# The last batch's two query tiles in the other order, in a two-layer transformer kernel

## The chip, the cores and the metric

The kernel runs on one NeuronCore of a Trainium2 chip. The metric is the device time of one execution in microseconds (us). The kernel before took 961.02 us (median of three runs, 960.78 to 964.9).

TensorE (PE) multiplies matrices; VectorE (DVE), ScalarE (ACT) and GpSimd (POOL) do elementwise work, and the queue of SyncE (SP) issues most of the DMAs. Everything is float32.

## What is computed

Two post-norm layers on x of 4 batches x 256 tokens x 512 features. After every attention and every feed-forward product the residual is added and the sum is normalised over its features.

```python
x = _layernorm(x + _L0_attn_ref(x, Wq, bq, Wk, bk, Wv, bv, Wo, bo))  # causal, 32 heads of 16, 8 KV heads
x = _layernorm(x + _L0_ffn_ref(x, q_scales, q_vals, bias))           # x @ W.T + bias, W = scale * (q - 128)
x = _layernorm(x + _L1_attn_ref(x, w_qkv, w_o))                      # causal, 32 heads of 128, 8 KV heads, bias -slope * sqrt(distance)
x = _layernorm(x + _L1_ffn_ref(x, kernel))                           # x @ w, w made of one int8 row of weights, 8 times
```

Attention is causal. The 256 queries of a batch are cut into two tiles of 128. Query tile 0 sees 128 keys, query tile 1 sees all 256: for a query tile qt, the width is w = (qt + 1) * 128.

## The kernel before

**Tiles.** The 1024 tokens are 8 token tiles of 128 rows; token tile 2 * b + qt holds query tile qt of batch b. x (first the input, later x2, the output of layer 0) lies in 8 slots of one pool.

**Layer 0, attention.** The helper `run` (L325) walks over 64 steps (b, qt, h, i): 4 batches, 2 query tiles, 2 halves of the KV heads, 4 query heads per group. A group of 8 steps makes one query tile. At step n, `run` traces in this order:
- `before0` (L543): at the first step of a batch, the projections of the next batch are appended to the list `ahead`; batch 3 has none.
- `begin0` (L475) of step n: scores sc on PE (L484), causal mask (DVE, L489), negated maximum (DVE, L492), four exponentials with their sums (ACT, L276); then `divide0` for the step before: reciprocal of the sums (DVE, L281) and the division of the probabilities pr (POOL, L284).
- `fill` (L556): one piece of every tail that is open, and one piece of `ahead`.
- `transpose0` (L508) of step n - 3: transposes of pr (PE, L299), one PSUM bank per 128 keys, each copied out to prT by ACT or DVE in turn (L102, L104). prT has 5 slots; a group of query tile 0 takes 2 of them, one of query tile 1 takes 4.
- `end0` (L524) of step n - 5: after the last step of a group, the output o (PE, L532, 16 matmuls per 128 keys), its copy oT, and a new tail.

**Layer 0, tails.** `tail0` (L436) takes a token tile through output projection py (L440), residual and statistics (L442, L259 to L262, the power on POOL), normalise (L266) to x1, transposes to x1T, bias addition (POOL, L453), feed-forward product pf (L457), residual and statistics (L461), normalise to x2, transposes to x2T. Between the steps it yields; two idle yields are left out for the last token tile (L448, L467).

**The border.** After step 63 `run` goes on without scores: the division of the last step, the last transposes, the last o. Then come the early projections of layer 1 (`first`, L739), which read only the first 512 tokens, while the last two tails end. The later projections need sums of the four quarters of x2T, made on POOL by `token_sums` (L599): all token columns but those of the last tile in one call (L744), held behind the newest power on POOL, and the last tile's columns in another (L697).

**Layer 1.** `run` walks over 64 steps (kv, b, qt), with transposes one step and o two steps after the scores. For the KV heads 0 to 6 the transposes go through DVE and DMAs. For the last one, kv = 7, they are on PE (L299), and each o leads to `output1` (L838: py, L842) and `tail1` (L771): residual, statistics, the sums xs of four quarters of features, their transpose, product pf (L797), z (L799), statistics, and the output. The output of the last token tile is written in two halves from two queues (L808 to L813), that of the others in one DMA (L818). After the last step a loop (L1066) ends what is open.

**What sets the order.** [...]The framework's scheduler fills the queues at compile time: roughly in the order in which the program traces the instructions, though an instruction that it takes to be ready earlier can move ahead. `keep_in_program_order` and `issue_after` pin some of them. The feed-forward weight of layer 0 comes as int32 codes (qv, L152) and is decoded in place (wf_n, L210). It lies in the pool `wa`, beside layer 0's other weights. The pool `w1` holds the weights of layer 1, its output weight wo1 in two slots.

Of the kernel before, what the change touches and what calls it, by code (L numbers as in the profile page):

```python
# [12 lines left out]
F32 = mybir.dt.float32  # L13
I32 = mybir.dt.int32
# [6 lines left out]
P = 128  # L21
B, S, D = 4, 256, 512
NTT = B * S // P
NC = D // P
NKV, G = 8, 4
BLK = 32
# [16 lines left out]

def alibi_slopes():
# [13 lines left out]
def block_kernel(  # L62
# [26 lines left out]
    const = pool(ctx, "const")  # L89
    xp = pool(ctx, "xp", NTT)  # L90
    w1 = pool(ctx, "w1", 2)
# [16 lines left out]
    xf = x_in.flatten_outer_dims()  # L108
    for tt in range(NTT):
        x.append(xp.tile([P, D], F32, tag="x", name=f"x_{tt}"))  # L110
# [7 lines left out]
    table = const.tile([P, 2 * P], F32, name="table")  # L118
    x2T = const.tile([P, NC, B * S], F32, name="x2T")

# [3 lines left out]
    wa = pool(la, "wa", side="right")  # L124
# [11 lines left out]
    def bank_m(name):  # L136
        return ps_w.tile([P, D], F32, tag="w", name=name)


    wq_n = x2T[:, :, 0:D]  # L140
    wq = wa.tile([P, NC, G, P], F32, name="wq")
    wk = wa.tile([P, NC, P], F32, name="wk")
    wv = wa.tile([P, NC, P], F32, name="wv")
    wop = w0.tile([P, G, D], F32, name="wop")
# [4 lines left out]
    bo_b = wa.tile([P, D], F32, name="bo_b")  # L149
    fb_b = w0.tile([P, D], F32, name="fb_b")  # L150
    brow = wa.tile([G + 1, P], F32, name="brow")
    qv = wa.tile([P, NC, D], I32, name="qv")  # L152
    qs = wa.tile([P, NC, D // BLK], F32, name="qs")
    wf_n = qv.bitcast(F32)

    tc.keep_in_program_order(nc.scalar.dma_start(wk, Wk.rearrange("(c p) n -> p c n", p=P)))
    tc.keep_in_program_order(
# [18 lines left out]
    nc.sync.dma_start(fb_b, f_bias.partition_broadcast(P))  # L176
    for tt in range(4, NTT):
        nc.sync.dma_start(x[tt], xf[ts(tt, P), :])
# [257 lines left out]
    def tail0(tt, oT):  # L436

        py = bank_m(f"py_{tt}")
        for i in range(G):
            nc.tensor.matmul(py, oT[:, i, :], wop[:, i, :], start=(i == 0), stop=(i == G - 1))  # L440
        y = s0.tile([P, D], F32, tag="y", name=f"y_{tt}")
        nc.vector.tensor_tensor(y, py, x[tt], ALU.add)  # L442
        factors = norm_factors(y, f"a{tt}")
        yield True
        x1 = s0.tile([P, D], F32, tag="x1", name=f"x1_{tt}")
        normalise(x1, y, factors)
        yield True
        if tt < NTT - 1:  # L448
            yield True
            yield True  # L450
        x1T = s0.tile([P, NC, P], F32, tag="x1T", name=f"x1T_{tt}")
        transposed(x1T, x1, f"x1_{tt}")
        nc.gpsimd.tensor_tensor(x1, x1, fb_b, ALU.add)  # L453
        yield True
        pf = bank_m(f"pf_{tt}")
        for c in range(NC):
            nc.tensor.matmul(  # L457
                pf, x1T[:, c, :], wfT[:, c, :], start=(c == 0), stop=(c == NC - 1)
            )
        y2 = s0.tile([P, D], F32, tag="y", name=f"y2_{tt}")  # L460
        nc.vector.tensor_tensor(y2, pf, x1, ALU.add)  # L461
        factors = norm_factors(y2, f"b{tt}")
        yield True
        x2[tt] = xp.tile([P, D], F32, tag="x", name=f"x2_{tt}")
        normalise(x2[tt], y2, factors)
        yield True
        if tt < NTT - 1:  # L467
            yield True
            yield True
        transposed(x2T[:, :, ts(tt, P)], x2[tt], f"x2_{tt}")  # L470
        yield True
# [36 lines left out]
    def transpose0(b, qt, h, i, pr):  # L508
        name = f"0_{b}_{qt}_{h}_{i}"
        if i == 0:  # L510
            open0[h] = [
                a0.tile(
                    [P, G, 4, 4, 32], F32, tag="prT", name=f"prT0_{b}_{qt}_{h}_{kt}", bufs=5
                )
                for kt in range(qt + 1)
            ]
        transposed_probabilities(
            name,
            pr,
            [(kt, open0[h][kt][:, i].rearrange("p j n q -> p n j q")) for kt in range(qt + 1)],  # L520
        )
        return open0[0], open0[1] if h else None
# [19 lines left out]

    def before0(step):  # L543
        b, qt, h, i = step
        if (qt, h, i) == (0, 0, 0):
            if b == 0:
                for _ in range(3):
                    advance(ahead)
            else:
                exhaust(ahead)  # L550
            if b + 1 < B:
                ahead.append(project0(b + 1))
            if b == 1:
                load_weights1(0)

    def fill():  # L556
# [3 lines left out]
    ahead.append(project0(0))  # L560
    tails.append(feed_forward_weight())
    run(
        [(b, qt, h, i) for b in range(B) for qt in range(2) for h in range(2) for i in range(G)],
        begin0,
        transpose0,
        end0,
# [15 lines left out]
    qk1 = {}  # L582
    v1 = a1.tile([P, NTT, NKV * P], F32, name="v1", bufs=1)

# [14 lines left out]
    def token_sums(start, end):  # L599
        B11, B21, B12, B22 = (  # L600
            x2T[:, 2 * j : 2 * j + 2, h * D + start : h * D + end]
            for h in range(2)
            for j in range(2)
        )
        t2_, t3_, t4_ = (xt[:, n, :, start:end] for n in range(3))
        nc.gpsimd.tensor_tensor(t3_, B22, B12, ALU.subtract)
        nc.gpsimd.tensor_tensor(B12, B12, B11, ALU.subtract)
        nc.gpsimd.tensor_tensor(t2_, B22, B12, ALU.subtract)
        return nc.gpsimd.tensor_tensor(t4_, B21, t2_, ALU.subtract)
# [59 lines left out]
    def project1(kv):  # L669

        wq1, _ = weights1[kv]
        parts = []
        if kv % 2 == 0:
            wk1 = wk_pair[kv // 2]
            nc.scalar.mul(wk1, wk1, scale)
            for e in range(2):
                kT1[kv + e] = a1.tile([P, B * S], F32, tag="kT1", name=f"kT1_{kv + e}", bufs=3)
            C = {(e, h): kT1[kv + e][:, ts(h, D)] for e in range(2) for h in range(2)}
            parts.append(Quarters(f"k_{kv}", halves(wk1, P, 0, P), None, C))
        qT = a1.tile([P, G, B * S], F32, tag="qT1", name=f"qT1_{kv}")  # L680
        for n in range(2):
            C = {(i, h): qT[:, 2 * i + n, ts(h, D)] for i in range(2) for h in range(2)}
            A = halves(wq1, P, n * P, (2 + n) * P)
            parts.append(Quarters(f"q_{kv}_{n}", A, None, C))

        def sums(part, where=p1):
            ws = where.tile([P, 4, 2, P], F32, tag="ws", name=f"ws_{part.name}", bufs=1)
            part.S = [ws[:, m] for m in range(4)]
            left_sums(part.S, part.A)

        if kv == 0:
            for part in parts:
                yield from part.early()
            sums(parts[0])
            for part in value_parts:
                yield from part.early()
            complete = token_sums(3 * P, D)  # L697
        for n, part in enumerate(parts):
            if kv > 0:
                sums(part)  # L700
                yield from part.early()
            yield from part.late()
            if kv == 0 and n == 0:
                with tc.issue_after(complete.ins):
                    sums(parts[1], border["pool"])
            elif kv == 0 and n + 1 < len(parts):
                sums(parts[n + 1])
            if kv == 0 and n == 0:
                with tc.issue_after(complete.ins):
                    left_sums(value_parts[0].S, value_parts[0].A)  # L710
            if kv == 0 and n > 0:
                yield from value_parts[n - 1].late()
        if kv == 0:
            yield from value_parts[2].late()
            yield from value_parts[3].late()
        qk1[kv] = (qT, kT1[kv])
        yield True
# [22 lines left out]
    for n in range(7):  # L740
        advance_all(tails)
        if n == 2:
            with tc.issue_after(powers[-1].ins):
                token_sums(0, 3 * P)  # L744
        next(first)
    exhaust(tails)
    l0.close()
# [23 lines left out]
    def tail1(tt):  # L771
# [33 lines left out]
        nc.gpsimd.tensor_tensor(rs, rs, minus_half, ALU.pow)  # L805
        yo = t1.tile([P, D], F32, tag="yo", name=f"yo_{tt}")
        rows = out.flatten_outer_dims()[ts(tt, P), :]
        if tt == NTT - 1:  # L808
            for part, queue in zip((ts(0, 2 * P), ts(1, 2 * P)), (nc.sync, nc.scalar)):
                nc.vector.tensor_scalar(  # L810
                    yo[:, part], z[:, part], mv[:, 0:1], rs, ALU.subtract, ALU.mult
                )
                queue.dma_start(rows[:, part], yo[:, part])  # L813
        else:
            shift = t1.tile([P, 1], F32, tag="shift", name=f"shift_{tt}", bufs=4)
            nc.gpsimd.tensor_scalar(shift, mv[:, 0:1], rs, -1.0, ALU.mult, ALU.mult)
            nc.scalar.activation(yo, z, AF.Identity, bias=shift, scale=rs)
            nc.sync.dma_start(rows, yo)  # L818
# [227 lines left out]
    def fill1():  # L1046
# [7 lines left out]
            advance(ahead)  # L1054

    run(
        [(kv, b, qt) for kv in range(NKV) for b in range(B) for qt in range(2)],
        begin1,
        transpose1,
        end1,  # L1060
# [42 lines left out]
```

## Time and profile before

| what | value |
|---|---|
| the three timed runs | 960.78, 961.02, 964.9 us |
| the profiled execution | 960.96 us |
| its span, first to last instruction | 958.8 us |
| around the span | 2.2 us |
| mean granted TensorE clock | 0.992 |
| first scores of batch 3, layer 0 | 195.66 us |
| first instruction of the last py of layer 0 | 266.41 us |
| last py of layer 1 begins | 944.48 us |

All places in the profile are us from the span's start. A row of the timeline has its start, its length, engine, line, operation, output <- inputs, shapes and count; a bracket at the end has the engine's idle time before it and what ended that. A row of a table by stage has a stretch, its length, the busy us of each engine and the granted clock (1.00 is full speed).

### The profile page before, as it was taken

The numbers are of one execution on the slowest core, as the hardware profiler recorded it, in microseconds if no ns is written. First come the engines' busy times: TensorE is split into PE (matmuls) and PEld (weight loads), VectorE is DVE, ScalarE is ACT, GpSimd is POOL, SyncE is SP. The second block draws the span as 40 slices with busy tenths as digits, with TensorE's granted clock in tenths as the row PEclk, the third lists the DMA queues.
The fourth block names the chain that finished last, engine by engine and source line by source line (L and its number), as shares of the span: only waits on it lengthen the run. The fifth ranks groups of instructions, "written<-read, shape, count | busy, mean of one in ns | idle before, by whom it ended". The sixth has DMA issues, their size and how long they took to land.

```text
span 958.8 us, 11377 instructions
## 1 busy us (share of the span) xinstructions
PE 922.0 (96%) x3593; PEld 554.1 (58%) x3593; DVE 619.4 (65%) x1291; ACT 315.2 (33%) x1194; POOL 445.6 (46%) x461
## 2 busy tenths in 40 slices
PE   8999999998899999999999999999999999999996
PEld 5655455553544445666666666666666666666652
DVE  4886777778533447655667666666676576666566
ACT  3674555466411003232222222212122122214441
POOL 3563553554457015445443543534543534556732
PEclk9999999999899999999999999999999999999998
DMA  8500000000020102444443353343344333432001
GB/s 242 184 1 1 0 1 1 1 1 1 1 88 22 45 0 72 128 115 126 110 135 86 112 152 99 121 125 95 117 125 111 115 83 110 126 94 69 1 34 55
DMA packets 76418, 74.45 MB, mean 78 GB/s; under 512 B 5957, under 2 KB 52678, under 8 KB 76358
## 3 DMA queue, kind: packets, MB, share of 16 engines
q1 hardware_dynamic: 75014, 72.02, 26.2%
q10 hardware_dynamic: 1344, 1.70, 0.6%
q8 instruction: 29, 0.48, 0.2%
q14 instruction: 31, 0.25, 0.1%
HBM read 49.58 MB, written 24.12 MB: 77 GB/s over the span
## 4 chain that ended last, share of the span: by engine, by line
PE 79%; POOL 9%; DVE 6%; ACT 2%; issue 1%; DMA 1%; ACTq 0%; POOLq 0%; DVEq 0%
PE p_q L632 18%; PE po L881 14%; PE sc L968 7%; PE o L1008 7%; PE p_k L632 5%; PE p_v L632 5%; PE sc L484 4%; PE pt L299 3%; PE py L440 3%; PE pf L457 3%; PE o L532 2%; PE pq L401 2%; POOL pr L284 2%; ACT pr L276 2%; PE py L842 2%; POOL x L903 2%
## 5 line engine op out<-in xcount | busy, mean ns | idle before, releaser
L276 ACT ACTIVATE pr<-sc,nm 128x256 f32<-128x256 f32 (+1 forms) x512 | 209.5, 421 | 362.2 <-DVE nm L984 277.2
L284 POOL TENSOR_TENSOR pr<-pr,sums 128x512 f32<-128x512 f32 (+1 forms) x128 | 190.4, 1489 | 231.2 <-DVE sums L281 220.9
L976 DVE SCALAR_TENSOR_TENSOR sc<-table,sc 128x128 f32<-128x128 f32 (+1 forms) x256 | 86.1, 356 | 34.7 <-PE sc L968 32.4
L276 ACT ACTIVATION_READ_ACCUMULATOR pr<-sc,nm 128x1 f32 x512 | 104.2, 203 | 0.0
L968 PEld LDWEIGHTS sc<-kT,qT 128*128 128x128 f32 x512 | 82.3, 191 | 35.1 <-issue 29.7
L968 PE MATMUL sc<-kT,qT 128*128 128x256 f32 (+1 forms) x512 | 95.0, 327 | 0.0
L1008 PE MATMUL o<-prT,v 128*128 128x512 f32 x192 | 92.9, 592 | 0.0
L310 DVE STREAM_TRANSPOSE blocks<-pr 128x512 f32<-128x512 f32 x84 | 57.6, 698 | 45.2 <-POOL pr L284 45.1
L646 DVE TENSOR_TENSOR qT<-p_q,qT 128x512 f32<-128x512 f32 x96 | 64.6, 686 | 33.6 <-PE p_q L632 32.8
L299 PE MATMUL pt<-ident,pr 128*128 128x128 f32 x432 | 64.3, 284 | 11.7 <-POOL pr L284 8.2
L299 PEld LDWEIGHTS pt<-ident,pr 128*128 128x128 f32 x432 | 50.7, 145 | 38.1 <-issue 19.9
L984 DVE TENSOR_REDUCE nm<-sc 128x2 f32<-128x512 f32 (+1 forms) x128 | 70.1, 551 | 1.5
L484 PE MATMUL sc<-kT,qT 32*128 32x256 f32 (+1 forms) x256 | 61.6, 532 | 2.8 <-ACT pr L276 2.7
L492 DVE TENSOR_REDUCE nm<-sc 128x4 f32<-128x512 f32 (+1 forms) x64 | 61.0, 954 | 1.2
L881 PE MATMUL po<-wo,so 128*128 128x256 f32 x224 | 58.0, 381 | 2.1 <-POOL so L612 2.1
L632 PE MATMUL p_q<-x2T,ws_q 128*128 128x512 f32 x128 | 59.8, 592 | 0.0
L489 DVE TENSOR_TENSOR sc<-sc,causal 128x512 f32<-128x512 f32 x64 | 44.4, 694 | 22.8 <-PE sc L484 22.5
L104 ACT COPY o<-o 128x512 f32<-128x512 f32 x29 | 17.0, 586 | 124.9 <-PE o L1008 124.9
L632 PE MATMUL p_q<-xt,ws_q 128*128 128x512 f32 x128 | 57.7, 592 | 0.0
L881 PE MATMUL po<-wo,o 128*128 128x256 f32 x224 | 57.7, 380 | 0.0
L632 PE MATMUL p_q<-x2T,wq 128*128 128x512 f32 x128 | 57.6, 592 | 0.0
L881 PE MATMUL po<-to,so 128*128 128x256 f32 x224 | 53.3, 381 | 1.0 <-POOL so L615 1.0
(155 smaller groups left out, 1410.2 us busy)
## 6 DMA issues: line engine op xcount, KB each, us to landing
way<-blocks SPq DMA_DIRECT2D x112, 128.0 KB, 2.5
prT<-way SPq DMA_DIRECT2D x28, 512.0 KB, 3.7
wq<-in_L_attn_w_qkv_dram SPq DMA_DIRECT2D x8, 1024.0 KB, 5.1
wo<-in_L_attn_w_o_dram SPq DMA_DIRECT2D x8, 1024.0 KB, 5.1
way<-blocks SPq DMA_DIRECT2D x112, 64.0 KB, 1.8
prT<-way SPq DMA_DIRECT2D x28, 256.0 KB, 2.6
wk<-in_L_attn_w_qkv_dram SPq DMA_DIRECT2D x4, 512.0 KB, 4.1
wv<-in_L_attn_w_qkv_dram SPq DMA_DIRECT2D x2, 1024.0 KB, 6.3
```

The lines of the kernel that those rows point to most:

```text
L276: nc.scalar.activation(pr[:, i, 0:w], sc, AF.Exp, bias=nm[:, i : i + 1], accum_out=sums[:, i : i + 1])
L284: nc.gpsimd.tensor_tensor(pr[:, :, 0:w], pr[:, :, 0:w], sums.unsqueeze(2).to_broadcast([P, G, w]), ALU.mult)
L299: nc.tensor.transpose(pt[:, i, :], pr[:, i, ts(kt, P)], ident)
L484: nc.tensor.matmul(sc[:, j, :, 0:w], qT[rows, i, ts(qt, P)], kT[rows, :, 0:w], start=True, stop=True)
L492: nc.vector.tensor_reduce(nm, scf[:, :, 0:w], AX.X, ALU.max, negate=True)
L632: nc.tensor.matmul(bank, fixed, moving, start=(c == 0), stop=(c == 1))
L646: add = lambda dst, a, b: nc.vector.tensor_tensor(dst, a, b, ALU.add)
L881: nc.tensor.matmul(bank[:, ts(n, HALF)], left[:, c, :], right[:, c, :], start=(c == 0), stop=(c == 1),)
L968: nc.tensor.matmul(sc[:, m, 0:w], qT[:, 2 * j + m, b * S + qt * P : b * S + (qt + 1) * P], kT[:, b * S : b * S + w], start=True, stop=True,)
L976: nc.vector.scalar_tensor_tensor(sc[:, m, 0:w], table[:, 2 * P - w :], slopes[kv * G + 2 * j + m], sc[:, m, 0:w], ALU.mult, ALU.add,)
L984: nc.vector.tensor_reduce(nm[:, 2 * j : 2 * j + 2], sc[:, :, 0:w], AX.X, ALU.max, negate=True)
L1008: nc.tensor.matmul(o, v1[:, 2 * b + kt, ts(kv, P)], prT[:, kt].rearrange("p j h q -> p h j q"), start=(kt == 0), stop=(kt == qt),)
```

## The change

For the last batch the two query tiles change places: in layer 0, and in layer 1 for the last KV head. Token tile 7 is then worked on before token tile 6, so everything that was tied to "the last token tile" is tied to tile 6 (`ENDING`): the idle yields, the output in two halves, and the columns of x2T that are summed last. The sums of the other columns are now two calls, of 256 columns (in each half of the tokens) and of 128. Two wide groups of layer 0 now follow each other, batch 2's and batch 3's; prT gets a sixth slot. To make room for it, the int32 weight moves from the pool `wa` to a slot of wo1 in `w1`.

```diff
+ENDING = NTT - 2
...
+def query_tiles(b):
+
+    return (1, 0) if b == B - 1 else (0, 1)
...
-    qv = wa.tile([P, NC, D], I32, name="qv")
+    wf_n = w1.tile([P, NC, D], F32, tag="wo1", name="wf_n")
+    qv = wf_n.bitcast(I32)
     qs = wa.tile([P, NC, D // BLK], F32, name="qs")
-    wf_n = qv.bitcast(F32)
...
-        if tt < NTT - 1:
+        if tt != ENDING:
...
-                    [P, G, 4, 4, 32], F32, tag="prT", name=f"prT0_{b}_{qt}_{h}_{kt}", bufs=5
+                    [P, G, 4, 4, 32], F32, tag="prT", name=f"prT0_{b}_{qt}_{h}_{kt}", bufs=6
...
-        if (qt, h, i) == (0, 0, 0):
+        if (qt, h, i) == (query_tiles(b)[0], 0, 0):
...
-        [(b, qt, h, i) for b in range(B) for qt in range(2) for h in range(2) for i in range(G)],
+        [(b, qt, h, i) for b in range(B) for qt in query_tiles(b) for h in range(2) for i in range(G)],
...
-            complete = token_sums(3 * P, D)
+            complete = token_sums(2 * P, 3 * P)
...
-                token_sums(0, 3 * P)
+                token_sums(0, 2 * P)
+                token_sums(3 * P, D)
...
-        if tt == NTT - 1:
+        if tt == ENDING:
...
-        [(kv, b, qt) for kv in range(NKV) for b in range(B) for qt in range(2)],
+        [
+            (kv, b, qt)
+            for kv in range(NKV)
+            for b in range(B)
+            for qt in (query_tiles(b) if kv == NKV - 1 else range(2))
+        ],
```

More of the change, by code (lines that the diff above doesn't have):

```diff
@@ L466, in tail0 @@
         yield True
-        if tt < NTT - 1:
+        if tt != ENDING:
             yield True
```

## The prediction

> **What bounds the kernel now.** I read the page first, then PE's waits, then the busy time by stage, then the timelines around the places where PE stands.
>
> ```profile
> PE 922.0 (96%) x3593; PEld 554.1 (58%) x3593; DVE 619.4 (65%) x1291; ACT 315.2 (33%) x1194; POOL 445.6 (46%) x461
> ```
>
> TensorE (PE) is busy 96% of the 958.8 us span. The change alters neither the number nor the shapes of its instructions, so a gain can only come out of the time in which PE stands or runs at a lower clock, near the places that are touched. PE's busy time by stage (columns: stretch, its length, busy us of PE, PEld, DVE, ACT, POOL, then granted clock):
>
> ```profile
> 195.66:266.41 70.75, 61.95 (x326) 31.51 (x325) 49.72 (x96) 39.74 (x156) 34.26 (x26) 0.95 0.00 1
> 266.41:876.00 609.59, 606.51 (x2073) 373.74 (x2074) 378.62 (x790) 138.20 (x522) 277.87 (x299) 1.00 0.36 101
> ...
> 936.00:959.00 23.00, 13.59 (x33) 5.56 (x32) 13.72 (x36) 4.67 (x9) 5.45 (x11) 0.88 0.16 58
> ```
>
> Two touched stages leave PE idle: batch 3 of layer 0 (195.66, its first scores, to 266.41, the output projection py of the last token tile), idle 8.80, and the last 23 us, idle 9.4. Between them PE is full, so whatever is saved before 266.41 arrives at the end whole. PE's waits up to 290 us:
>
> ```profile
> PE pt L299 <- POOL pr L284: 6.2, 4, 2.6
> ...
> PE sc L484 <- ACT pr L276: 2.7, 5, 0.7
> ```
>
> All four of the first lie in batch 3. Two are in the middle, two further on; PE's timeline has them (last bracket: idle before, and the releaser):
>
> ```profile
> 218.77 0.66 PE L299 MATMUL pt<-ident,pr 128*128 128x128 f32 x4
> 221.05 0.66 PE L299 MATMUL pt<-ident,pr 128*128 128x128 f32 x4 [1.62 <-POOL pr L284]
> ...
> 224.54 0.66 PE L299 MATMUL pt<-ident,pr 128*128 128x128 f32 x4 [1.34 <-POOL pr L284]
> ```
>
> ```profile
> 247.79 1.09 PE L299 MATMUL pt<-ident,pr 128*128 128x128 f32 x8
> 251.48 1.97 PE L299 MATMUL pt<-ident,pr 128*128 128x128 f32 x8 [2.60 <-POOL pr L284]
> 253.27 1.12 PE L272 MATMUL pt_x<-ident,x 128*128 128x128 f32 x4
> 254.18 1.91 PE L299 MATMUL pt<-ident,pr 128*128 128x128 f32 x8
> 256.12 4.29 PE L457 MATMUL pf<-wfT,x1T 128*128 128x512 f32 x8
> ...
> 261.95 3.64 PE L532 MATMUL o<-prT,v 128*32 128x512 f32 x32 [0.68 <-ACT prT L104]
> 266.41 3.70 PE L440 MATMUL py<-wop,oT 128*128 128x512 f32 x8 [0.81 <-DVE oT L102]
> ```
>
> The reader should see two costs in the second: the 2.60 wait, and after it the same eight transposes take 1.97 instead of 1.09. The clock shows why:
>
> ```profile
> 247.10:250.50 3.40, 1.78 (x12) 0.86 (x8) 3.40 (x6) 1.13 (x5) 0.97 (x1) 1.00 0.02 5
> 250.50:257.40 6.90, 5.90 (x22) 4.77 (x23) 3.40 (x7) 4.77 (x16) 5.29 (x4) 0.51 0.00 0
> ```
>
> PE was busy 5.90 us there at half speed, a loss of 2.95. By rows: transposes +0.9 and +0.9, pt_x +0.5, pf +0.7, in all 3.0. **Lost in batch 3:** waits of 0.71, 0.18, 1.62, 1.34, 0.61, 0.22, 2.60, 0.68, 0.81 make 8.77; with 2.95 it is 11.7 us.
>
> **What the Trainium skill says.** "TensorE: Matmul & The Clock Gate", section "What's actually happening": the clock falls to half after a window of 3413 ns, free-running, in which PE was idle, and returns after a busy one. The trace agrees in length (6.90, two windows; 114.0 to 117.4 at 0.50, one) and shows that half idle is enough: windows with PE busy 1.78 and 1.99 of 3.40 were followed by half clock, one with 2.06 (223.2 to 226.6) was not. The same page, "Architectural detail", has VectorE's queue strictly in order. It agrees: the exponentials of the tile that PE waits for at 251.48 ended at 243.8, but their reciprocal L281 ran at 249.20. It was queued behind a normalise L266, which waited for POOL, behind the next step's mask, an evacuation and the next maximum, so the division on POOL came at 249.53.
>
> **Layer 0, the order.** A group is the 8 steps of one query tile. A step issues scores (PE), mask and maximum (DVE), exponentials (ACT); its reciprocal and division (DVE, POOL) come after the next step's maximum; its transposes follow three steps later. No step issues a DMA. PE per step: scores 1.06 and transposes about 0.98 at 256 keys, 0.63 and 0.53 at 128. Moving the wide group first puts 8 x (0.43 + 0.45) us of PE work early and takes it from the end: PE's sum is unchanged. What changes is which waits remain.
> - The batch's start: the 0.71 wait is for a score bank that the exponentials of two steps before give back at 198.6. Wide scores cover 0.43 of it, but the change to narrow steps now stands in the middle of the batch and has a like wait. I keep **0.7**.
> - The middle (1.62 + 1.34): it follows the 3.6 us py of batch 2's last tile, which holds back the next scores. With wide tiles the chain grows by 0.53 (maximum 1.13 against 0.60) and 0.86 (division 1.90 against 1.04), with scores 0.43; the PE work inside it grows from 3.5 to 5.6. The first wait is then about 0.9 if DVE keeps that order, 2.6 if it takes the order of the end (normalise first): **1.7**. The second: **0.5** (0 to 1.0).
> - The small ones (0.18, 0.61, 0.22) belong to wide steps behind a long matmul group; narrow ones there: **0.2**.
> - The end. Steps 6 to 8 of the last group, now narrow, are the same sequence as the narrow steps at 216 to 222 (py, transposes, scores, x2T, transposes): their wait was 1.62, so **1.6** in place of 2.60. The next transposes then need a division that at 223.45 stood behind the bias addition L453 (1.26 on POOL); with no more scores to fill PE, that costs up to 2.4, nothing if the tile's feed-forward product pf (3.4) goes first. I take **0.4**.
> - Evacuation of prT, then of oT, ahead of o and py: same operations, 0.68 + 0.81 now, **1.4**. The last o has 16 matmuls instead of 32, but the other 16 moved earlier.
> - Clock: with no wait over 1.7 I take **0** for half clock.
> After: 0.7 + 2.2 + 0.2 + 1.6 + 0.4 + 1.4 = 6.5 against 11.7, a saving of **5.2 us**.
>
> **Buffers.** With two wide groups in a row, four prT tiles are live when two more are asked for: six. With five, a wait that the kernel doesn't have now would appear; with six, 0. The integer weight takes one of the two slots of the output weight wo1. Both wo1 loads are issued at 24.1 to 25.8 now; the second must then wait on SP's queue until the weight's last transpose (L222, 38.7). Behind it on that queue stands the load L724, issued at 270.3, and its own reader comes in layer 1: 0. The x slots: tile 7's x2 is now made before x of tile 6 is read. If it got that slot, its normalise (L465) would wait on DVE for L442 of tile 6, and DVE's queue behind it; x2T of tile 7 has, as tile 6's now, the early projections from 266.4 to 298.7 as cover: 0.
>
> **Sums of tokens on POOL.** Before the last tile: 4 x 1.81 = 7.2 becomes 4 x 1.27 (the 512-wide addition L453) + 4 x 0.73 = 8.0, so +0.8 (as low as -0.1, since the first four no longer wait for the copy of x2T, 274.0 to 274.6). Behind them on POOL is L453, which ended at 283.4, and DVE's L461 needs it at 284.8: slack 1.4 covers it; without that cover, 0.8. After the last tile: 4 x 0.73 as before. **0.**
>
> **Layer 1's end.** PE works without a gap from 916.2 to 942.6, so the order in that stretch moves nothing: wide scores, transposes and o come a step earlier (+0.86, +0.43, +0.86) and the sum is equal. The wide tile's division must end before its transposes: now its scores start at 918.39 and it ends at 927.35, 9.0 later; one step earlier it has 10.4 us of PE work as cover, slack 1.4. The last tile's chain (py, sum, statistics, xs, transpose, pf, z, statistics, output on two queues) has the same lengths. The 0.35 wait at 916.18 for a score bank may become 0 to 0.8. **0**, from -0.4 to +0.5. The two idle yields and the split output only follow the last tile: 0.
>
> **Sum.** The profiled execution took 960.96 (median of the three runs 961.02, so it is typical): 960.96 - 5.2 = **955.8 us**.
>
> **Rivals.**
> - *A better case:* PE's queue has tile 7's x1T and pf ahead of the starved transposes, and the middle wait is 0.9. Lost: 0.7 + 0.9 + 0.2 + 0.3 + 1.4 = 3.5, so 952.8. For it: in the middle, pf is already interleaved with scores (225.03). Against it: at 254.18 transposes still go ahead of pf.
> - *The gain is given back at the end:* the second wait is 2.4 and trips the clock for one window: 6.5 + 2.0 + 1.7 = 10.2, so 959.5. For it: narrow steps give PE only 3.4 us of work where the chain takes 5.1; at 221 to 224.5 the trace has such a pair.
> - *Slower, starvation of PE by narrow steps:* DVE takes the normalise first in both places. Then the middle loses 2.6 + 1.0 and the end 3.45 (chain 8.2 - 0.53 - 0.86 = 6.8, PE work 3.35) + 2.4, and each trips two half-clock windows: 0.7 + 3.6 + 0.2 + 5.85 + 1.4 + 5.9 = 17.7, so 966.9. It decides once the two clock losses exceed 5.2. Against it: in the narrow group of the trace DVE had the maximum first.
>
> **Chances.** Forecast 0.50, better 0.13, given back 0.26, slower 0.11. 0.5% (4.8 us), about what a measurement can tell from no change here, lies at 956.2 and 965.8. Of the forecast's own spread (plus or minus 2) 0.35 lies below 956.2; with the better case 0.48 faster. Of the slower case 0.07 is beyond 965.8. The rest, 0.45, is within. The range takes in the better case and the given-back one with its own spread: 952.5 to 962.5.
>
> **What would show it.** Right: no half clock between batch 3's start and the last py, and PE's idle there near 6.5. The middle waits and the end wait for POOL's L284 show the three terms by themselves. Wrong: a half-clock stretch before the last o, or a wait over 2 for L284 near the end. Wrong altogether: a gain of another size in layer 1's end, whose py to output rows should be unchanged.

## The result and the profile after

The kernel after took **965.35 us** (median of 22 runs, 960.68 to 967.35), the kernel before 961.3 (22 runs beside it, 958.07 to 965.95). The ratio is 1.003, 95% interval 1.0016 to 1.0045: slower by 0.3%, some 3 us (the medians lie 4.05 apart), where 5.2 us faster was forecast, and above the range. It lies within the 0.5% that was called "about what a measurement can tell" beforehand, but the many runs put the whole interval above 1. The profiled execution of the kernel after took 966.16 us with a span of 964.4, so it stands 0.8 above its median, and the two profiles differ by 5.6 in span, more than the medians do.

Line numbers are now 6 higher in layer 0 and 7 higher in layer 1: the division on POOL is L290 (L284 before), the transposes L305, the normalise L272, the negated maximum L498, the bias addition L459.

First the page's line of busy times:

```profile
PE 925.8 (96%) x3593; PEld 556.4 (58%) x3593; DVE 620.6 (64%) x1291; ACT 315.2 (33%) x1194; POOL 446.1 (46%) x465
```

PE has the same 3593 instructions, but they took 3.8 us more than before (925.8 against 922.0). The same work became slower. Next the table by stage (columns as in the prediction: stretch, length, busy us of PE, PEld, DVE, ACT, POOL, granted clock); the last five rows are the clock's windows around the two places where PE stands:

```profile
195.83:270.47 74.64, 65.09 (x326) 33.42 (x325) 50.17 (x96) 39.88 (x156) 34.08 (x26) 0.89 0.00 1
...
223.10:226.47 3.37, 1.41 (x10) 0.86 (x8) 3.37 (x7) 1.48 (x7) 1.32 (x1) 1.00 0.00 0
226.47:236.71 10.24, 9.61 (x32) 6.06 (x32) 5.74 (x11) 6.39 (x26) 6.47 (x5) 0.50 0.00 1
...
253.77:257.19 3.42, 1.33 (x10) 0.76 (x9) 2.83 (x8) 2.15 (x10) 1.80 (x2) 1.00 0.00 0
257.19:264.02 6.83, 4.43 (x15) 3.00 (x14) 2.15 (x5) 2.04 (x9) 3.09 (x3) 0.50 0.00 0
```

Batch 3 of layer 0, from its first scores to its last py, lasts 74.64 us instead of 70.75: **+3.9**. With the same 326 PE instructions, PE is busy 65.09 instead of 61.95 (+3.1) and idle 9.55 instead of 8.80 (+0.75). So four fifths of the loss in this stage is PE running slower: before, one stretch of 6.90 us ran at half speed, now two of 10.24 and 6.83. At full speed that work took 61.95 - 2.95 = 59.0 before, which puts the clock's price after at 6.1 us; half of the busy time in the two stretches, 9.61 / 2 + 4.43 / 2, gives 7.0. Each stretch follows a window in which PE was busy 1.41 or 1.33 of 3.4 us.

The rows of PE's timeline at both places (start, length, engine, line, operation, tiles, shapes, count, and in the bracket the idle time before and its releaser):

```profile
223.42 1.09 PE L305 MATMUL pt<-ident,pr 128*128 128x128 f32 x8
227.10 1.54 PE L305 MATMUL pt<-ident,pr 128*128 128x128 f32 x6 [2.59 <-POOL pr L290]
228.57 1.22 PE L490 MATMUL sc<-kT,qT 32*128 32x256 f32 x4
...
254.20 0.66 PE L305 MATMUL pt<-ident,pr 128*128 128x128 f32 x4
256.95 0.92 PE L305 MATMUL pt<-ident,pr 128*128 128x128 f32 x4 [2.09 <-POOL pr L290]
257.66 1.06 PE L278 MATMUL pt_x<-ident,x 128*128 128x128 f32 x4
261.12 1.11 PE L305 MATMUL pt<-ident,pr 128*128 128x128 f32 x4 [2.40 <-POOL pr L290]
262.02 4.59 PE L463 MATMUL pf<-wfT,x1T 128*128 128x512 f32 x8
```

Before, one wait was over 2 us (2.60); now three are: 2.59 in the middle, where the wide tile's last steps meet the tail of batch 2, and 2.09 and 2.40 at the end. DVE's timeline in the middle shows who is late:

```profile
222.02 0.55 DVE L272 TENSOR_SCALAR x<-y,mv_a,rs_a 128x512 f32<-128x512 f32 x1 [0.66 <-POOL rs_a L268]
222.49 0.69 DVE L495 TENSOR_TENSOR sc<-sc,causal 128x512 f32<-128x512 f32 x1
223.09 0.68 DVE L108 COPY prT<-pt 128x512 f32<-128x512 f32 x1
223.68 1.21 DVE L498 TENSOR_REDUCE nm<-sc 128x4 f32<-128x1024 f32 x1
224.81 0.17 DVE L287 RECIPROCAL sums<-sums 128x4 f32<-128x4 f32 x1
```

The normalise, which had to wait for POOL's power, stands ahead of mask, copy and maximum, and the reciprocal of the tile that PE wants comes last, at 224.81. That is the sequence which made the 2.60 wait before, moved into the middle. At the end POOL's queue has a part in it:

```profile
255.64 1.25 POOL L290 TENSOR_TENSOR pr<-pr,sums 128x512 f32<-128x512 f32 x1 [0.22 <-DVE sums L287]
258.80 1.26 POOL L459 TENSOR_TENSOR x<-x,fb_b 128x512 f32<-128x512 f32 x1 [1.91 <-PE pt_x L278]
260.02 1.04 POOL L290 TENSOR_TENSOR pr<-pr,sums 128x512 f32<-128x512 f32 x1
```

The wait of 2.09 is for the division at 255.64, whose reciprocal ended on DVE at 255.47. The division for the transposes of 261.12 stood behind the bias addition, which had itself waited for pt_x, which ran at half speed. That is only a part of the 2.40: the reciprocal for this division ended at 259.28, so POOL's queue held it up by 0.74. The reciprocal itself was late on DVE, where its maximum stood behind a copy (257.90) that had waited 1.30 for the transposes of 256.95, also at half speed.

The rest of the span gives +0.17 ahead of the batch, +0.8 between the last py of layer 0 and that of layer 1 (678.87 against 678.07), and +0.7 after it, where some is a half-clock window that falls otherwise in the last, idle microseconds. Of the +0.8, 0.5 comes back below in every profile of the new order that leaves the tails as they are. By the traces it belongs to the split token sums. The first call of `token_sums` no longer waits for the last copy of x2T, so it starts on POOL 0.07 us before a normalise on DVE. That normalise then took 1.48 us, where it took 0.55 before. The rows of POOL, DVE and PE after:

```profile
277.78 1.27 POOL L612 TENSOR_TENSOR xt<-x2T 128x512 f32<-128x512 f32 x1
277.85 1.48 DVE L272 TENSOR_SCALAR x<-y,mv_a,rs_a 128x512 f32<-128x512 f32 x1 [1.82 <-POOL rs_a L268]
279.98 1.98 PE L638 MATMUL p_q<-x2T,wq 128*128 128x512 f32 x4 [0.22 <-DVE kT L647]
```

The first two before, the other way round:

```profile
273.79 0.55 DVE L266 TENSOR_SCALAR x<-y,mv_a,rs_a 128x512 f32<-128x512 f32 x1 [1.82 <-POOL rs_a L262]
274.68 1.81 POOL L606 TENSOR_TENSOR xt<-x2T 128x768 f32<-128x768 f32 x1 [0.93 <-ACT x2T L104]
```

The copy kT behind the normalise comes later, and PE waits for it. From the last py of layer 0 to the first product of layer 1 that needs the sums it takes 32.81 us instead of 32.32.

### The profile page after: what moved, and what is told of

Its sections match the earlier page's. It is cut to its first block, busy times and chain, and to the rows that moved or that the text cites. A ratio compares the mean times of both kernels' runs of the same rounds, so it can differ in the third digit from the quotient of the medians.

```text
span 964.4 us, 11383 instructions
## 1 busy us (share of the span) xinstructions
PE 925.8 (96%) x3593; PEld 556.4 (58%) x3593; DVE 620.6 (64%) x1291; ACT 315.2 (33%) x1194; POOL 446.1 (46%) x465
## 4 chain that ended last, share of the span: by engine, by line
PE 79%; POOL 9%; DVE 7%; ACT 2%; issue 1%; DMA 1%; ACTq 0%; POOLq 0%; DVEq 0%
PE p_q L638 18%; PE po L888 14%; PE sc L975 7%; PE o L1015 7%; PE p_v L638 5%; PE p_k L638 5%; PE sc L490 4%; PE pt L305 3%; PE pf L463 3%; PE py L446 3%; PE pq L407 2%; ACT pr L282 2%; POOL pr L290 2%; PE py L849 2%; PE o L538 2%; POOL x L910 2%
## 5 line engine op out<-in xcount | busy, mean ns | idle before, releaser
L290 POOL TENSOR_TENSOR pr<-pr,sums 128x1024 f32<-128x1024 f32 (+1 forms) x128 | 190.2, 1487 | 235.5 <-DVE sums L287 231.1
L975 PE MATMUL sc<-kT,qT 128*128 128x128 f32 (+1 forms) x512 | 95.0, 327 | 0.0
L305 PE MATMUL pt<-ident,pr 128*128 128x128 f32 x432 | 64.9, 285 | 12.6 <-POOL pr L290 9.1
L305 PEld LDWEIGHTS pt<-ident,pr 128*128 128x128 f32 x432 | 50.5, 145 | 40.5 <-issue 20.6
L991 DVE TENSOR_REDUCE nm<-sc 128x2 f32<-128x256 f32 (+1 forms) x128 | 69.9, 550 | 1.5
L498 DVE TENSOR_REDUCE nm<-sc 128x4 f32<-128x512 f32 (+1 forms) x64 | 61.0, 952 | 1.1
```

The source lines that it names most:

```text
L290: nc.gpsimd.tensor_tensor(pr[:, :, 0:w], pr[:, :, 0:w], sums.unsqueeze(2).to_broadcast([P, G, w]), ALU.mult)
L305: nc.tensor.transpose(pt[:, i, :], pr[:, i, ts(kt, P)], ident)
L498: nc.vector.tensor_reduce(nm, scf[:, :, 0:w], AX.X, ALU.max, negate=True)
L975: nc.tensor.matmul(sc[:, m, 0:w], qT[:, 2 * j + m, b * S + qt * P : b * S + (qt + 1) * P], kT[:, b * S : b * S + w], start=True, stop=True,)
L991: nc.vector.tensor_reduce(nm[:, 2 * j : 2 * j + 2], sc[:, :, 0:w], AX.X, ALU.max, negate=True)
```

## The experiments

**Theory A:** the change loses in batch 3 of layer 0, because PE stands long enough in two places for the clock to fall, and it falls for longer than before. **Rival B:** the loss is elsewhere: layer 1's order, the split token sums, or the moved buffers. **Rival C:** the order itself is worse, whatever the clock does. Each kernel was timed beside the kernel before.

### Which part of the change costs

*Layer 0 alone:* the kernel after with layer 1's order and its last tile put back.

```diff
-        if tt == ENDING:
+        if tt == NTT - 1:
...
-            for qt in (query_tiles(b) if kv == NKV - 1 else range(2))
+            for qt in range(2)
```

> The changed kernel with layer 1 put back: the two query tiles of the last KV head in the old order, token tile 7 written last. Layer 0's new order, the sixth prT slot and the moved integer weight stay. Theory A (the loss is made in batch 3 of layer 0, where narrow steps at the end and the step after a long product leave PE waiting for divisions, and the TensorE clock halves after that): the loss stays, 963 to 967 us, with waits of PE for L290 of about 2.6, 2.1 and 2.4 us and half clock after the first and the last of them. Theory B (the loss is layer 1's): back to 960 to 962. Theory C (the loss is the integer weight's new place): as A in time, but PE's stage from batch 3's first scores to the last py no longer than the 70.8 us of the kernel before.

Measured 965.43 (962.88 to 966.51), ratio 1.004 [1.0025, 1.0055]. Its waits and its two half-clock stretches (10.24 and 6.83 us) are those of the kernel after. The whole loss comes with the layer-0 part of the change, which here includes the moved buffers and the split token sums.

*Layer 1 alone:* the kernel before with the last KV head's order and the split output moved.

```diff
-        if tt == NTT - 1:
+        if tt == NTT - 2:
...
-        [(kv, b, qt) for kv in range(NKV) for b in range(B) for qt in range(2)],
+        [(kv, b, qt) for kv in range(NKV) for b in range(B) for qt in ((1, 0) if (kv, b) == (NKV - 1, B - 1) else (0, 1))],
```

> The kernel before with the change in layer 1 alone: the last batch's two query tiles of the last KV head change places and token tile 6 is written last. Theory A (layer 0): no loss here, within 1 us of the kernel before. Theory B (layer 1): 2 to 4 us slower, with the difference after 876 us.

Measured 961.27 (958.18 to 968.0), ratio 1.001 [0.9993, 1.0026]: nothing that can be measured, as forecast.

*Buffers alone:* the kernel before with the weight in the slot of wo1 and six slots for prT.

```diff
-    qv = wa.tile([P, NC, D], I32, name="qv")
+    wf_n = w1.tile([P, NC, D], F32, tag="wo1", name="wf_n")
+    qv = wf_n.bitcast(I32)
...
-                    [P, G, 4, 4, 32], F32, tag="prT", name=f"prT0_{b}_{qt}_{h}_{kt}", bufs=5
+                    [P, G, 4, 4, 32], F32, tag="prT", name=f"prT0_{b}_{qt}_{h}_{kt}", bufs=6
```

> The kernel before with the buffers' edit alone: the integer weight in a slot of wo1, six prT slots; the instructions stand in the same order on every engine. Theory A: no difference, within 1 us. Theory C (the weight's place costs, since the load of the second wo1 tile now waits on SP and the start looks 1.8 us later in the changed kernel's profile): 1.5 to 2 us slower, all of it before 50 us.

Measured 960.45 (957.65 to 965.23), ratio 0.9998 [0.9979, 1.0017]: nothing. In the trace of the kernel after, SP's two issues of the load of wo1 did take 17.3 us instead of 1.65, most of it a wait for the integer weight, and this run shows no cost for it. So layer 1's order and the buffers are out. The split token sums were not run alone. The stretch of 32.32 us after the last py of layer 0 is 32.80 or 32.81 in the profiles of the kernel after, of layer 0 alone, and below of the five slots and of the four runs with filler in the new order; in layer 1 alone and buffers alone it is 32.32. So rival B falls but for some 0.5 us, which the traces put down to the split sums.

*The sixth slot:* the kernel after with five.

```diff
-                    [P, G, 4, 4, 32], F32, tag="prT", name=f"prT0_{b}_{qt}_{h}_{kt}", bufs=6
+                    [P, G, 4, 4, 32], F32, tag="prT", name=f"prT0_{b}_{qt}_{h}_{kt}", bufs=5
```

> The kernel after with five slots for the transposed probabilities instead of six. The prediction says that a wait appears which six slots do not have: the copy of the transposes then waits for an output o of four steps before. If that wait reaches PE, 965.3 + 0.5 to 3, so 966 to 968.5. Rival (the output comes before the copy in any case, the sixth slot is not needed): 965.3 within 1 and the same waits as the kernel after.

Measured 964.71 (960.52 to 967.75), ratio 1.003 [1.0012, 1.0048]: under the 966 to 968.5 that were expected if the wait reached PE in full. It appears, and it is small. PE's waits in batch 3 (engine, tile and line, releaser: us in total, times, longest):

```profile
PE pt L305 <- POOL pr L290: 7.1, 3, 2.6
...
PE pt L305 <- DVE prT L108: 0.3, 1, 0.3
```

The second row (0.26 us at 208.8) is absent with six slots. The prediction's wait exists, but no loss of time can be measured: the sixth slot wasn't needed.

### Is it the clock?

*Filler in all three places:* extra transposes of the identity ahead of the starved ones, into the same PSUM bank, which the real transposes then overwrite. They compute nothing; they keep PE busy.

```diff
+            for _ in range({("0_3_1_1_1", 0): 16, ("0_3_0_1_1", 0): 14, ("0_3_0_1_2", 0): 14}.get((name, kt), 0)):
+                nc.tensor.transpose(pt[:, 0, :], ident, ident)
```

> The changed kernel with work added that computes nothing: 16, 14 and 14 transposes of the identity on PE, into the bank that the three starved transposes are about to overwrite, ahead of these. That is about 1.9, 1.7 and 1.7 us of PE work inside waits of 2.59, 2.09 and 2.40, so the transposes themselves start no earlier. If the half clock after the waits is a cost of its own (4.8 us in the middle, 2.2 at the end of the profile), PE's clock stays full in batch 3 and the kernel gets 4 to 7 us faster although it does more: 958.5 to 961.5. If the waits alone make the loss, it stays at 964 to 967, or gets slower by up to 5 where the added work is in the way.

Measured **957.99** (956.39 to 959.47), ratio 0.9961 [0.9948, 0.9974]: 7.4 us below the kernel after, though PE does some 5 us more work. It is also below the kernel before, and a little under the expected 958.5 to 961.5. By stage:

```profile
195.11:262.95 67.84, 63.10 (x369) 34.28 (x368) 50.16 (x96) 39.80 (x156) 33.93 (x26) 1.00 0.00 1
...
222.80:226.21 3.41, 1.75 (x15) 1.51 (x15) 3.41 (x6) 1.94 (x9) 1.78 (x1) 1.00 0.02 5
226.21:229.63 3.42, 3.37 (x26) 2.54 (x27) 2.61 (x6) 3.42 (x16) 2.12 (x3) 1.00 0.00 0
```

The clock is 1.00 throughout batch 3, which lasts 67.84 us instead of 74.64. One caution for the middle: the filler also changed the order there. The scores of the next step now stand between two parts of the filler, and PE waits 1.70 for their bank in place of 2.59 for the division:

```profile
223.63 0.93 PE L305 MATMUL pt<-ident 128*128 128x128 f32 x7
226.26 0.70 PE L492 MATMUL sc<-kT,qT 32*128 32x256 f32 x4 [1.70 <-ACT pr L282]
226.89 1.20 PE L305 MATMUL pt<-ident 128*128 128x128 f32 x9
```

*Filler in the middle alone, and at the end alone:*

```diff
+            for _ in range({("0_3_1_1_1", 0): 16}.get((name, kt), 0)):
+                nc.tensor.transpose(pt[:, 0, :], ident, ident)
```

> The kernel after, with 16 extra 128x128 transposes of the identity (they compute nothing that is used) ahead of the starved transposes in the middle of batch 3 only; the end of batch 3 stays starved. Theory A (half clock after a long wait is what the change lost, and the two places add up): the middle's half clock, 10.24 us costing about 4.8, is gone and the end's 6.83 us stays, so about 960.5 (959.5 to 961.5), 4 to 5.5 below the kernel after. Rival B (the places are coupled: with the middle early the end is starved more): 962 to 964. Rival C (the filler helps by moving the order of instructions and not by the clock): 958 or 965, whichever place the move is in.

```diff
+            for _ in range({("0_3_0_1_1", 0): 14, ("0_3_0_1_2", 0): 14}.get((name, kt), 0)):
+                nc.tensor.transpose(pt[:, 0, :], ident, ident)
```

> The kernel after, with 14 + 14 extra transposes of the identity ahead of the two starved transposes at the end of batch 3 only; the middle stays starved. Theory A: the end's half clock, 6.83 us costing about 2.2, is gone and the middle's 10.24 us stays, so about 963 (962 to 964). Together with the run that fills the middle only, its gain should make the 7.4 of the run that fills both. Rival B (coupled places): gain under 1 or over 4. Rival C (order of instructions): no half clock missing at the end though the time falls.

The middle alone gave 960.87 (959.82 to 965.35), ratio 0.9994 [0.9979, 1.001], 4.5 below the kernel after; the end alone 961.78 (957.66 to 963.54), ratio 1.0 [0.9987, 1.0013], 3.6 below. The end brought a little more than expected (962 to 964). The sum, 8.1, is near the 7.4 of both together, so the two places nearly add up. In its profile each removes the half clock at its own place and leaves it at the other (6.83 us at the end in the first, 6.83 in the middle in the second). The end is the clean case, since no other instruction moved there:

```profile
252.82 0.66 PE L307 MATMUL pt<-ident,pr 128*128 128x128 f32 x4
253.31 1.69 PE L305 MATMUL pt<-ident 128*128 128x128 f32 x14
255.57 0.66 PE L307 MATMUL pt<-ident,pr 128*128 128x128 f32 x4 [0.57 <-POOL pr L290]
256.07 0.60 PE L278 MATMUL pt_x<-ident,x 128*128 128x128 f32 x4
256.51 1.69 PE L305 MATMUL pt<-ident 128*128 128x128 f32 x14
258.03 0.60 PE L307 MATMUL pt<-ident,pr 128*128 128x128 f32 x4
```

From the end of the transposes before (253.5) to the end of the second starved ones (258.6) it takes 5.2 us; in the kernel after, the same stretch (254.9 to 262.2) takes 7.4. The filler stands inside the waits, and the real rows run in 0.60 to 0.66 instead of 0.92 to 1.11.

*Half of the filler:*

```diff
+            for _ in range({("0_3_1_1_1", 0): 8, ("0_3_0_1_1", 0): 7, ("0_3_0_1_2", 0): 7}.get((name, kt), 0)):
+                nc.tensor.transpose(pt[:, 0, :], ident, ident)
```

> The kernel after, with half of the filler in all three places (8, 7 and 7 transposes of the identity): the waits of 2.59, 2.09 and 2.40 become about 1.6, 1.25 and 1.55. If a wait of that size, lying in one window of 3.41 us, still trips half clock (windows with PE busy 1.78 and 1.99 did, 2.06 and 2.15 did not), it depends on how the window falls: 958 to 963 with a wide spread between runs. Theory A1 (a threshold near half idle): 958 to 960. Rival A2 (any wait over 1.2 us trips it): 963 to 965.5, with 10 us or more of half clock in batch 3.

Measured **957.99** (957.09 to 959.0), ratio 0.995 [0.993, 0.997]: the same as with all of it. It fits the 958 to 960 of the threshold theory, and the rival that any wait over 1.2 us trips the clock falls: PE still stands 1.71 us at one place, in a window in which it is busy 2.01 of 3.41 us. Its stage:

```profile
196.13:263.52 67.39, 61.33 (x348) 31.70 (x347) 50.23 (x96) 39.75 (x156) 33.98 (x26) 1.00 0.00 1
```

Idle is 67.39 - 61.33 = 6.06 at full clock. This looks like what the prediction described for the kernel after (6.5 lost, no half clock), but the filler fills a part of the waits: against the 59.0 us or so that the work alone takes at full clock, 8.4 us are still lost.

*Filler in the kernel before*, ahead of its one wait of 2.60, as a fair comparison of the two orders:

```diff
+            for _ in range({("0_3_1_1_1", 0): 16}.get((name, kt), 0)):
+                nc.tensor.transpose(pt[:, 0, :], ident, ident)
```

> The kernel before with 16 transposes of the identity on PE ahead of the transposes that wait 2.60 us at 251.5 and are followed by half clock (6.8 us in the first profile, 3.4 in two later ones of the same order of instructions). With the clock as a cost of its own: no half clock there, 1.7 to 3 us faster, 958 to 959.5. Without: 961 or slightly slower.

Measured 959.02 (956.92 to 964.8), ratio 0.9984 [0.9967, 1.0002]; in the profile there is no half clock in batch 3:

```profile
194.22:263.09 68.87, 60.85 (x341) 31.08 (x340) 49.81 (x96) 39.66 (x156) 34.16 (x26) 1.00 0.00 1
```

With the clock full in both, the new order's stage is 1.0 us shorter (67.84 with filler, against 68.87). But 0.8 of it is given back by the last py of layer 1 (678.72 us after the last py of layer 0, against 677.90), 0.5 of that where the token sums stand. Nor do the times show a gain. The two medians, 957.99 and 959.02, are not both at full clock: five of the 22 executions of this run, at 963.18 to 964.8, have a mean granted clock of 0.990 to 0.992, where the other 17 have 0.995 to 0.997 and a median of 957.6. The profiled executions took 957.38 here and 958.09 in the new order. Rival C falls: with the clock kept up the order is not worse by more than about 0.7 us. It isn't measurably better either.

### Can the order be mended without filler?

*Fewer idle yields in the tails*, so that normalise, transposes and pf of tiles 5 and 7 are traced earlier and could fill PE. First both pairs of yields, in the kernel after:

```diff
-        if tt != ENDING:
+        if tt not in (5, 6, 7):
...
-        if tt != ENDING:
+        if tt not in (5, 6, 7):
```

> The changed kernel with the two idle yields of layer 0's tails left out for token tiles 5 and 7 too, so that their x1 transposes and feed-forward products (3.4 us of PE each) stand on PE ahead of the transposes that were starved. Theory A: the waits for L290 at about 227, 257 and 261 shrink to under 1 us each, no half clock remains in batch 3, and the time falls by 6 to 11 us against the changed kernel, to 954 to 959. A rival, that PE's order is no matter because the chain through DVE and POOL is the bound: the waits move to other places, the sum of PE's waits in batch 3 stays near 9.5 us, and the time stays within 2 us of the changed kernel.

Measured 963.06 (960.52 to 965.01), ratio 1.0023 [1.0011, 1.0034]: missed. The waits for POOL's division are gone and others stand in their place:

```profile
PE pt_x L278 <- DVE x L272: 6.1, 3, 2.8
PE pf L463 <- DVE x1T L108: 1.2, 1, 1.2
```

The transposes of x2 were now ahead of their normalise. All waits in batch 3 sum to 9.5 us, as in the kernel after: so far the rival in the expectation was right, that the waits only move. Then the first pair alone:

```diff
-        if tt != ENDING:
+        if tt not in (5, 6, 7):
```

> The changed kernel with only the first pair of idle yields (ahead of the transposes of x1) left out for token tiles 5 and 7; the second pair, ahead of the transposes of x2, stays. In the run that left out both pairs PE no longer waited for divisions (L290) but 1.55, 1.75 and 2.79 us for the normalise to x2, whose transposes had come two steps early. If PE's order decides (theory A), these three waits go too, nothing over 1.3 us is left in batch 3 but the evacuations ahead of the last o and py, no half clock remains, and the time is 954 to 958. If the chain through DVE and POOL is the bound (the rival), waits of about 5 us in sum turn up elsewhere and the time stays at 962 to 964.

Measured 960.72 (958.74 to 961.88), ratio 0.9995 [0.9982, 1.0007]. It is 4.6 us below the kernel after, short of the expected 954 to 958 but below the rival's 962 to 964: its waits sum to 7.1, the longest is 1.75, and half clock lasted one window (3.41 us at 253.05). The same step in the kernel before, for tiles 5 and 6:

```diff
-        if tt < NTT - 1:
+        if tt not in (5, 6, 7):
```

> The kernel before with the first pair of idle yields left out for token tiles 5 and 6: the same repair of PE's order, with the old order of query tiles. It tells whether the new order of query tiles is worth anything once PE is fed. Theory A: waits of 2.60, 1.62 and 1.34 mostly gone, no half clock in batch 3, 955 to 958. If the narrow tile at the end has its own worth (a shorter last division, half the last o moved early), the repaired changed kernel is ahead of this one by 1 to 2 us; if not, they are equal within 1 us.

Measured 967.9 (965.9 to 971.04), ratio 1.0068 [1.004, 1.0096]: missed, and the slowest of all.

```profile
PE pt L299 <- POOL pr L284: 3.2, 1, 3.2
PE pf L457 <- ACT x1T L104: 2.9, 1, 2.9
```

Two waits near 3 us brought half clock for 10.24 and 3.41 us. So one kind of edit to the tails gave 4.6 us in one kernel and cost 6.6 in the other: it moves the waits. The longest wait alone does not decide: in the run before this one it was 1.75, but with the waits around it PE was busy only 1.49 us of the window ahead of the half clock.

## Why the prediction was wrong

It failed in a named step: "**Clock: with no wait over 1.7 I take 0 for half clock.**" Of the profiled execution:

| term of the sum | forecast | found |
|---|---|---|
| batch's start | 0.7 | 0.48 |
| the middle, first wait | 1.7 (0.9 or 2.6) | 2.59 |
| the middle, second wait | 0.5 | 0 |
| the small ones | 0.2 | 0.50 |
| the end | 1.6 | 2.09 |
| the end, second wait | 0.4 (up to 2.4) | 2.40 |
| evacuations of prT and oT | 1.4 | 1.48 |
| half clock | 0 | 6.1 to 7.0 |
| lost in batch 3 | 6.5 | 15.6 to 16.5 |

- **The waits** came out 3.0 us longer (9.54 against 6.5). For the middle the prediction had both orders of DVE's queue, 0.9 and 2.6, and took the middle between them; DVE took the second, and the wait was 2.59. (The 0.9 leaves out the 0.43 of the longer scores; with them its sum gives 1.3.) For the second end wait it named the division behind the bias addition on POOL and took 0.4. The wait was 2.40, its upper bound, but that agreement is in part luck: POOL's queue made 0.74 of it, and the rest came over DVE from transposes at half clock. A mean between two orders is a time that neither order gives. For a sum of small terms that does little harm; ahead of a threshold it hides the case that decides.
- **The clock** cost 6 to 7 us and not 0. This is the term that turned the sign. The prediction had the evidence: it read that half idle trips the clock and quoted windows for it. It then applied that to single waits of its central values, where the windows count all idle in 3.41 us, and gave the upper bounds of its two waits, 2.6 and 2.4, their half clock in its rivals alone. Even its central value was not safe by its own figures: a wait of 1.7 that falls into one window leaves PE busy at most 1.71 of 3.41 us, less than the 1.78 after which it had seen the clock fall. That waits of 1.7 did not trip it in the three runs with filler in the middle of the new order was not known then. Section "What's actually happening" of "TensorE: Matmul & The Clock Gate" in the Trainium skill, on which it rested, agrees in the length of the windows (stretches of 3.41, 6.83 and 10.24 are one, two and three of them); but the return doesn't always follow the first busy one: in the kernel after PE was busy all of 229.88 to 233.29, and the next window still ran at half.
- **The rival "starvation of PE by narrow steps"**, 966.9 with 0.11, comes nearest: two places, a clock loss of 5.9, 17.7 lost. It was right in the middle (normalise first, 2.6). At the end DVE had the maximum first, as its counter-argument said, and POOL's queue and the half clock did the rest. It should have had more weight, since one of two unknown orders, in either place, is enough for a half-clock stretch. The prediction says that this case decides once its two clock losses exceed 5.2. That holds for the forecast's waits of 6.5; with this rival's own waits of 11.75 any clock loss makes the kernel slower, and with the 9.54 that were found 2.2 is enough.
- **Right:** the buffers cost nothing that can be measured, and neither does layer 1's end (0.9998 and 1.001). That five slots would bring a wait was right, at 0.26 us.
- **The token sums** were put at 0, with a slack of 1.4 us on POOL as the reason, and by the traces they cost 0.5. The prediction had seen that the first sums would start earlier. It had not asked what else runs at that moment: the normalise on DVE, which then took 1.48 us instead of 0.55.
- **The gain of the order by itself**, with the clock full in both kernels, is 1.0 us in batch 3 and nothing measurable in the whole. The prediction's sum without its 2.95 for the clock says 8.8 - 6.5 = 2.3.

What stays open: how much of the middle's recovery is the filler and how much the scores that moved with it, which no run separates; and why half clock lasted three windows at 226.47 in the kernel after, but two at the same wait in the runs with the end filled and with five slots. Also open is why the normalise lengthens beside POOL's sum, and the remaining 0.3 of the 0.8 after batch 3. An order that keeps every wait short without filler wasn't found; the nearest took 960.72.

## What to carry to other kernels

When a change moves waits about on a full TensorE, don't add up the waits alone: lay the 3.4 us windows over each place and ask how much idle one of them can gather. Here up to 1.26 us never tripped the clock, 1.85 or more always did, and how the windows fall isn't known beforehand. If one of two possible orders can reach that, forecast that order as a case of its own, with its half clock, and not a mean of the two. Where a wait can't be removed, a few useless matmuls ahead of it can be worth more than a better order: here 7.4 us, against 4.6 for the best order that was found.

## What the runs showed of the hardware

- **More work, less time.** 22 useless transposes (some 2.6 us of PE) took 7.4 us off; 44 of them took no more off.
- **Where the clock falls.** Windows of 3.41 us, laid from each half-clock stretch over the first 300 us of the profiles of before, after and the runs above, show: where the clock was full, PE busy up to 1.56 of 3.41 us was always followed by half clock (14 windows), 2.15 and more never; from 1.71 to 2.12 both happened. Around the wait of 1.7 in the middle, busy 1.75 (with all the filler, shown above) and 1.71 did not trip it, while 1.78 around the wait of 2.60 in the kernel before did:

```profile
223.75:227.17 3.42, 1.71 (x16) 1.47 (x15) 3.42 (x6) 1.99 (x9) 1.83 (x1) 1.00 0.02 5
251.06:254.47 3.41, 1.32 (x12) 0.99 (x10) 2.37 (x7) 2.09 (x9) 1.81 (x2) 1.00 0.00 0
254.47:261.30 6.83, 4.43 (x10) 2.27 (x9) 1.90 (x5) 2.10 (x9) 3.31 (x3) 0.50 0.00 0
```

  These are windows of the run with only the middle filled: the first at full clock and followed by full clock, the second followed by the half clock of the third.
- **The spread of the runs goes with the clock.** After the same wait of 2.60, half clock lasted 6.83 us in the profile of the kernel before and 3.41 in those of the layer-1 and buffer runs, whose batch 3 has the same order and the same waits for POOL; PE was busy 1.75 us of the window that holds most of this wait in the first, 1.03 and 1.02 in the others. The kernel before ranged over 957.55 to 966.25 in 43 runs: the 12 with a mean granted clock of 0.990 or less took 962.74 to 966.25, the 31 with 0.992 or more 957.55 to 962.47. The kernel after with filler in three places, full or half, ranged over 956.39 to 959.47 and 957.09 to 959.0. Filler in the kernel before narrowed it less (956.92 to 964.8). Waits of 1.62 and 1.34 are left in its batch 3; that they trip the clock in its five slow executions, whose mean clock is lower, is likely but not shown, since only one execution was profiled.
- **A normalise on DVE beside a sum on POOL.** It took 1.48 us where POOL's sum of 1.27 us had started 0.07 us before it, 2.02 where one of 1.80 us had (the kernel before with fewer yields), and 0.55 in the kernel before, where the sum started 0.89 us after it.
